# Repeated targets of a graph kernel's scatters: merged window by window instead of once at the end

## The chip, the cores and the metric

The kernel runs on one core of one Trainium2 chip. The metric is device time in microseconds, from the start of the program to its end. The profile shows one execution on that core, with one row for each instruction of TensorE (PE, with its weight loads PEld), VectorE (DVE), ScalarE (ACT), GpSimd (POOL) and SyncE (SP, which issues most DMAs here).

## The reference

One layer of a graph network over 6,250 nodes with 128 features and 200,000 edges. Every edge has a source row `idx_i = src`, a neighbour `idx_j = dst` (sorted), 20 attributes and a weight.

```python
h = maximum(layernorm(x), 0)
xw = h @ W_in
W_ij = (ssp(f_ij @ W_f1 + b_f1) @ W_f2 + b_f2) * f_ij_cutoff   # ssp(v) = softplus(v) - log 2
x_ij = xw[idx_j] * W_ij                                         # one row of 128 per edge
out = segment_sum(x_ij, idx_i, 6250)
return x + ssp(out @ W_o1 + b_o1) @ W_o2 + b_o2
```

The gather by `dst` is easy, since `dst` is sorted. The sum by `src` is the work of this case: `src` is random, and 200,000 rows of 512 bytes have to be added into 6,250 rows.

## The kernel before

**Iterations.** Edges come in chunks of 128 and quads of four chunks; there are 391 quads. The program is written out as one long list of iterations, `for i in range(...)` (L1125); in iteration `i` quad `i` gets its first layer, quad `i-1` its second, and so on. Besides this regular work, hooks are placed by hand: `at(i, point, function, ...)` (L912) puts a call into iteration `i` at one of the points `L` (loads, first), `D0`, `D1`, `A0`, `A1`, `DM`, `PE2`, `A2`, `D2` and `S` (scatters, last). Each engine then has its instructions in exactly this order, and waits on semaphores where another engine is late.

**The regular part.** `s1_pe` is the first layer on PE; `s1_exp` and `s1_ln` its softplus on ACT; `s1_guard` (L447, DVE) makes the activation `a`; `s2_pe_x` and `s2_pe_w` are the gather as a one-hot product (`xg`) and the second layer (`W`, L470); `s2_copy` (L475, ACT) makes `xc`; `s2_m` (L485, DVE) multiplies the two to the edge rows.

**Three ways to sum by `src`.** 168 of the quads are *sorted*: their rows are permuted into 16 groups on PE (`permute`) and summed into an accumulator in SBUF (`unit_pe`, a burst of 96 matmuls in the iterations called units). Rows that do not fit a group go to an overflow tile, two quads of which are summed and scattered by `over_...` (`over_scatter`, at point `S`). The other 223 quads are *scattered*: GpSimd issues one indirect DMA with add for each chunk of 128 rows (`scatter`, L547), into one of four accumulators in DRAM (`acc0` to `acc3`, taken in turn). [...]

- *Plain* quads (the first 12 and the last 19 scattered ones) compare all pairs (`s1_eq`), add repeats up on PE (`s3_pe`), copy the sums out (`s3_copy`, ACT), and send all but one of each to a trash row.
- *Listed* quads (192, numbers `LB = 12` to `LE = 204` among the scattered ones) do without that. For a window of `SW = 16` quads (64 chunks; 12 windows) the kernel compares one window ahead: `l_eq` (L364, DVE) compares two quads at a time, `l_count` (L373, PE, point `PE2`) counts with falling weights, `l_dup` marks every row that repeats an earlier one of its chunk. `l_index` (L383) then numbers the marked rows of each partition with a running sum that goes on from window to window, and gives the `j`-th marked row of partition `p` the target `ACC_R + 128 (j-1) + p`: a row in a list of `LCAP = 24` blocks of 128 rows behind each accumulator. So the scatter of a listed chunk never hits a row twice.

**The merges.** Behind the listed quads the 24 blocks are added into their real rows. `l_id(j)` (L403, DVE, one pass over 768 columns) finds which node each row of block `j` belongs to. Then, for one block an iteration: `l_dg` (ACT) and `over_row` (PE, L696) spread the ids over a row, `l_same` (L423, DVE) compares, `l_load` brings the block of all four accumulators (four DMAs on SP), `l_sum` (L429, L430, PE) adds what belongs to the same node, `l_copy` (L435, ACT) puts it into an `os` tile (two buffers, shared with the overflow), `l_ji` (L440, L441) and `over_int` (L720) make the index, and `over_scatter` scatters 128 rows. The first block is started at iteration `lend + 8 = 368`, the last scattered at 401; the last quad is number 390. Rows beyond the 24 blocks would set a flag (`l_drop`), and their chunks would be done over behind the loop.

**What is zeroed.** The lists (25 blocks with a trash block, 3,200 rows behind each accumulator) are zeroed in the first 20 iterations by 20 DMAs on SP (`zero_list`), beside the accumulators themselves.

**The end.** The last 64 scatters leave out `acc0`, so that it can be added into SBUF early (`r0_load`, `r0_tp`, `r0_add`). Behind the loop the other three accumulators are loaded (L1265), added up, and the output layer runs over 13 groups of rows.

Of the kernel before, what the change touches and what calls it, by code (L numbers as in the profile page):

```python
# [7 lines left out]
F32 = mybir.dt.float32  # L8
BF16 = mybir.dt.bfloat16
# [11 lines left out]
P = 128  # L21
# [16 lines left out]
LCAP = 24  # L38
LR = P * (LCAP + 1)
# [15 lines left out]
def tile_gnn(ctx: ExitStack, tc: tile.TileContext, x, fB, cT, srcT, srcr, dstr, win_, wf1, wf2, bias, bo1c, wo1,  # L55
# [22 lines left out]
    ZL = 5  # L78
# [15 lines left out]
    for j in range(LCAP if LE else 0):  # L94
        scat[lend + 10 + 5 * j // 4] += 1
# [62 lines left out]
    lrow = con[:, 15:16]  # L158
# [200 lines left out]
    jd_all = dropT[:, 4 * LB:4 * LE]  # L359
# [22 lines left out]

    def l_index(w):  # L383
        n0 = 4 * (LB + SW * w)
        dup = lst.pop(("dup", w))
        j = sp_.tile([P, 4 * SW], F32, tag="lj", name="lj", bufs=2)
        first = lst["j", w - 1][:, 4 * SW - 1:] if w else 0.0
        nc.vector.tensor_tensor_scan(j, dup, dup, first, op0=ALU.add, op1=ALU.max)
        lst["j", w] = j
        u = sp_.tile([P, 4 * SW], F32, tag="lu", name="lu", bufs=1)  # L390
        nc.vector.tensor_scalar(u, j, float(P), float(P * (LCAP + 1)), op0=ALU.mult, op1=ALU.min)
        nc.vector.scalar_tensor_tensor(u, u, lrow, dup, op0=ALU.add, op1=ALU.mult)
        ji = sp_.tile([P, 4 * SW], I32, tag="lji", name="lji", bufs=2)
        nc.vector.tensor_tensor(ji, u, srcT_sb[:, n0:n0 + 4 * SW], op=ALU.max)
        lst["ji", w] = ji
        nc.vector.tensor_tensor(jd_all[:, 4 * SW * w:4 * SW * (w + 1)], j, dup, op=ALU.mult)

    def l_drop():
        nc.vector.tensor_scalar(jd_all, jd_all, float(LCAP), None, op0=ALU.is_gt)

    def l_id(j):
        t = wk.tile([P, 4 * (LE - LB)], BF16, tag="pr", name="lsel", bufs=1)
        nc.vector.scalar_tensor_tensor(t, jd_all, float(j + 1), srcT_sb[:, 4 * LB:4 * LE], op0=ALU.is_equal,  # L403
                                       op1=ALU.mult, accum_out=idl[:, j:j + 1])
# [396 lines left out]
    with tc.manual_schedule():  # L801
# [102 lines left out]
        idl = cp.tile([P, LCAP], F32, name="idl")  # L904
# [7 lines left out]
        def at(i, point, fn, *a):  # L912
            hooks.setdefault((i, point), []).append((fn, a))
# [133 lines left out]
        for w in range((LE - LB) // SW):  # L1047
            for g in range(4):
                n = LB + SW * (w - 1) + 4 * g
                i = splain[n] + 2 if w else 6 + 2 * g  # L1050
                for k in range(2):
                    kk = (LB + SW * w + 4 * g) // 2 + k
                    at(max(0, i + k - 2), "L", sb_load, kk)
                    at(i + k, "DM", l_eq, kk)
                i = clear(i + 1, units)
                at(i, "PE2", l_count, (LB + SW * w) // 4 + g)
                at(i + 1, "D0", l_dup, w, g)
            at(i + 1, "D0", l_index, w)
            last_i = i + 1
        if LE:  # L1060
            for k in range(NACC):
                for j in range(ZL):
                    at((0, 5, 10, 15)[k] + j + 1, "L", zero_list, k, j)
            at(last_i + 3 + LCAP, "D2", l_drop)
            for j in range(LCAP):
                at(last_i + 2 + j, "D2", l_id, j)
                i = clear(lend + 8 if j == 0 else i + 1, units)
                assert last_i + 2 + j < i
                at(i, "L", l_start, j)
                at(i, "A0", l_dg, j)  # L1070
                at(i, "PE2", over_row, ("L", j))
                at(i + 1, "D0", l_same, j)
                k = clear(i + 1, units)
                at(k - 1, "L", l_load, j)
                at(k, "PE2", l_sum, j)
                at(k + 1, "A0", l_copy, j)
                at(k + 1, "DM", l_ji, j)
                at(k + 1, "A2", over_int, ("L", j))
                at(k + 1, "S", over_scatter, ("L", j))
        for q in mpq:  # L1080
# [19 lines left out]
            if mpi[q] % 2 or q == mpq[-1]:  # L1100
# [10 lines left out]
                at(k + 1, "S", over_scatter, q)  # L1111
        last = mpq[-1]
        for r in range(len(mpq) // RND):
            for s, k in enumerate(unit_slots(mpq, r)):
# [6 lines left out]
                  l_count, l_sum)  # L1121
# [3 lines left out]
        for i in range(max(NQ + 7, last + 14, r0_end + 2, lend + 60)):  # L1125
# [262 lines left out]
def clear(i, busy, n=1):  # L1388
    while any(i + k in busy for k in range(n)):
        i += 1  # L1390
    return i
# [30 lines left out]
def _layout(inputs):  # L1422
# [27 lines left out]
    con[:, 15] = np_ + lane  # L1450
# [53 lines left out]
```

## Time and profile before

| what | us |
|---|---|
| three runs | 2256.68, 2262.07, 2265.48 (median 2262.07) |
| the profiled execution | 2264.35 |
| its span, first to last instruction | 2262.4 |
| PE, DVE, ACT, POOL busy | 1938.6, 1840.8, 1721.4, 1661.8 |
| mean granted TensorE clock | 0.944 of full speed |

An engine's row in a grouped view gives the source line, the engine, the operation, output and inputs, the count; then busy time in us and the mean of one in ns; then how long the engine had been idle just before, and whose end released it. A wait row says which engine and line waited for which, and then total us, number of waits, longest.

### The profile page before, as it was taken

The numbers are of one execution on the slowest core, as the hardware profiler recorded it, in microseconds if no ns is written. First come the engines' busy times: TensorE is split into PE (matmuls) and PEld (weight loads), VectorE is DVE, ScalarE is ACT, GpSimd is POOL, SyncE is SP. The second block draws the span as 40 slices with busy tenths as digits, with TensorE's granted clock in tenths as the row PEclk, the third lists the DMA queues.
The fourth block names the chain that finished last, engine by engine and source line by source line (L and its number), as shares of the span: only waits on it lengthen the run. The fifth ranks groups of instructions, "written<-read, shape, count | busy, mean of one in ns | idle before, by whom it ended". The sixth has DMA issues, their size and how long they took to land. (4 is left out here: it accounts for less than half of the span.)

```text
span 2262.4 us, 58115 instructions
## 1 busy us (share of the span) xinstructions
PE 1938.6 (86%) x20425; PEld 1342.8 (59%) x20425; DVE 1840.8 (81%) x4566; ACT 1721.4 (76%) x4509; POOL 1661.8 (73%) x1052
## 2 busy tenths in 40 slices
PE   3588889989898998888898999889998989988766
PEld 2456566666566666666665666666665656666644
DVE  4678889888888988979889798897987999966544
ACT  3578778878887878878788888788887888866514
POOL 3678888877777777776777787787787787666664
PEclk9789999999999999999999999999999999999987
DMA  7897666665656565656665666665656665565558
GB/s 244 229 233 135 108 119 122 114 125 100 117 110 118 104 130 103 122 110 116 116 115 102 115 112 106 111 119 98 127 100 115 109 102 99 111 110 112 98 84 228
DMA packets 390983, 279.94 MB, mean 124 GB/s; under 512 B 98815, under 2 KB 350122, under 8 KB 390690
## 3 DMA queue, kind: packets, MB, share of 16 engines
q0 software_dynamic: 145456, 72.09, 31.9%
q1 hardware_dynamic: 244946, 204.05, 31.2%
q8 instruction: 161, 2.64, 0.5%
q14 instruction: 132, 1.08, 0.2%
q10 hardware_dynamic: 288, 0.07, 0.0%
HBM read 157.60 MB, written 118.44 MB: 122 GB/s over the span
## 5 line engine op out<-in xcount | busy, mean ns | idle before, releaser
L547 POOL DMA_INDIRECT acc<-s,lji x768 | 1247.0, 1624 | 291.5 <-issue 179.6
L652 PE MATMUL pq<-pt,pm 128*128 128x387 bf16 x2688 | 552.2, 350 | 46.6 <-DVE pt L641 17.4
L475 ACT ACTIVATE xc<-xg,cb 128x128 f32<-128x128 f32 x1564 | 446.1, 372 | 85.3 <-PE xg L462 68.9
L470 PE MATMUL W<-w,a 128*128 128x128 f32 x3128 | 469.7, 295 | 0.1
L746 PE MATMUL un<-so,mst 32*128 32x392 bf16 x8064 | 390.7, 331 | 60.0 <-ACT os L711 33.8
L658 ACT CAST mst<-pq 128x387 bf16<-128x387 f32 x672 | 299.6, 480 | 158.2 <-PE pq L652 137.8
L470 PEld LDWEIGHTS W<-w,a 128*128 128x128 f32 x3128 | 393.8, 198 | 43.2 <-issue 4.5
L652 PEld LDWEIGHTS <-pm 128*128 128x128 bf16 x2688 | 265.9, 101 | 248.6 <-issue 47.1
L746 PEld LDWEIGHTS <-mst 32*128 32x128 bf16 x8064 | 245.3, 94 | 199.4 <-issue 112.9
L447 DVE SCALAR_TENSOR_TENSOR a<-z,e 128x512 f32<-128x512 f32 x391 | 266.2, 681 | 56.6 <-ACT e L319 46.1
L319 ACT ACTIVATE e<-e,con 128x512 f32<-128x512 f32 x391 | 282.3, 722 | 12.7
L547 POOL DMA_INDIRECT acc<-os,oji x108 | 174.4, 1615 | 156.0 <-ACT pt L647 118.4
L547 POOL DMA_INDIRECT acc<-s,ji x123 | 198.9, 1617 | 103.1 <-ACT ji L528 45.7
L313 ACT ACTIVATE e<-z 128x512 f32<-128x512 f32 x391 | 239.9, 614 | 28.9 <-PE z L308 18.6
L314 ACT ACTIVATE e<-e 128x512 f32<-128x512 f32 x391 | 246.4, 630 | 12.4
L641 DVE TENSOR_TENSOR pt<-pt 128x512 f32<-128x512 f32 x336 | 231.7, 690 | 5.8
L627 DVE TENSOR_SCALAR pm<-iot,pos 128x576 bf16<-128x576 f16 x672 | 220.6, 389 | 0.0
L757 DVE TENSOR_TENSOR accT<-un,accT 128x392 f32<-128x392 f32 x320 | 158.5, 557 | 65.5 <-PE xg L462 34.8
L485 DVE TENSOR_TENSOR s<-W,xc 128x512 f32<-128x512 f32 x192 | 131.6, 685 | 83.7 <-ACT xc L475 59.6
L731 DVE TENSOR_SCALAR so<-iot,mst 128x392 bf16<-128x392 f16 x672 | 190.8, 343 | 7.7 <-PE un L746 7.7
L308 PE MATMUL z<-ft,ws 123*128 123x512 bf16 x391 | 152.1, 390 | 30.0 <-DVE mo L903 9.0
L462 PE MATMUL xg<-wn,oh 63*128 63x128 bf16 x1564 | 158.7, 223 | 13.8 <-DVE a L447 7.0
(183 smaller groups left out, 2726.8 us busy)
## 6 DMA issues: line engine op xcount, KB each, us to landing
rb<-reld SPq DMA_DIRECT2D x391, 64.0 KB
fsd<-f SPq DMA_DIRECT2D x49, 480.0 KB
ft<-fsd SPq DMA_DIRECT2D x195, 120.0 KB
sb<-src SPq DMA_DIRECT2D x169, 128.0 KB
fb<-in_fB_dram SPq DMA_DIRECT2D x49, 320.0 KB
ft<-fsd SPq DMA_DIRECT2D x195, 80.0 KB
acc<-accT SPq DMA_DIRECT2D x40, 320.0 KB
wn<-tab SPq DMA_DIRECT2D x782, 15.8 KB
```

The costliest lines, as they stand in the source:

```text
L313: nc.scalar.activation(e, st[q]["z"], AF.Abs)
L314: nc.scalar.activation(e, e, AF.Exp, scale=-1.0)
L319: nc.scalar.activation(e, e, AF.Ln, bias=half, scale=0.5)
L447: nc.vector.scalar_tensor_tensor(a, st[q]["z"], 0.0, st[q]["l"], op0=ALU.max, op1=ALU.add)
L470: nc.tensor.matmul(W[:, c, :], st[q]["a"][:, c * P:(c + 1) * P], w2, start=False, stop=(c == 3))
L475: nc.scalar.mul(xc[:, c, :], st[q]["xg"][:, c, :], late["c", q // CQ][:, 4 * (q % CQ) + c:4 * (q % CQ) + c + 1])
L547: nc.gpsimd.indirect_dma_start(out=accs[k][:rows, :], out_offset=bass.IndirectOffsetOnAxis(ap=ji, axis=0), in_=s, in_offset=None, compute_ ...
L627: nc.vector.tensor_scalar(pm[:, c], iot[:, :SLOTS], rk[r]["pos"][:, 4 * j + c:4 * j + c + 1], None, op0=ALU.is_equal)
L641: nc.vector.tensor_tensor(pt[:, :, k * P:(k + 1) * P], a, high(a), op=ALU.subtract)
L652: nc.tensor.matmul(t[:, :PW], mp[q]["pm"][:, c, s * P:(s + 1) * P], high(mp[q]["pt"][:, c:c + 1, :PW])[:, 0], start=(c == 0), stop=(c == 3))
L658: nc.scalar.copy(mp[q]["ms", s][:, :PW], mp[q].pop(("q", s))[:, :PW])
L746: nc.tensor.matmul(ts[g][:, :GN], mp[q]["ms", s][v, k * P:(k + 1) * P], mp[q]["oh"][v], start=(q == qs[0] and k == 0), stop=(q == qs[-1] a ...
```

## The change

Every window of 16 listed quads now has one block of its own, of 128 rows, that is filled without gaps, and is merged soon after the window is scattered.

- *Numbering.* `l_scan` sums the marks of a window along each partition, from zero in each window; `l_before` adds up on PE (a triangular matrix times the partitions' totals) how many marked rows the partitions before have; the row is the sum of both. `l_index` keeps a row in the block if the block has room (128 rows) and the partition has at most `LCAP = 7`; others go to the trash row and set the flag.
- *Ids.* `l_id(w)` picks a partition's marked ids, seven passes over 64 columns; `l_place` puts them in their places in the block with seven matmuls against a shifted one-hot (`oh`), in two parts of bfloat16; `l_take` adds the parts up.
- *Merges.* Twelve instead of 24, by the same functions, the merge of a window started 12 iterations after its last quad (iterations 56 to 372), its scatter at 59 to 375. A window's scatters declare only the rows up to their own block, and later windows' blocks lie lower.
- *Lists.* 12 blocks, zeroed by 12 DMAs in the first 12 iterations.
- *One iteration later* stand `l_count` (with `l_dup`) and every `over_scatter`, those of the sorted quads' overflow included. `l_index` of a window stands one to two iterations later than before.

The diff, without the constants that only follow from it:

```diff
-LCAP = 24
-LR = P * (LCAP + 1)
+LCAP = 7
...
-    ZL = 5
+    ZL = 3
...
-    for j in range(LCAP if LE else 0):
-        scat[lend + 10 + 5 * j // 4] += 1
+    NW = (LE - LB) // SW
+    LR = P * NW
+    wend = [splain[LB + SW * (w + 1) - 1] for w in range(NW)]
+    for w in range(NW):
+        scat[wend[w] + 16] += 1
...
+    def l_base(w):
+        return ACC_R + P * (NW - 1 - w)
...
+    def l_scan(w):
+        dup = lst["dup", w]
+        j = sp_.tile([P, 4 * SW], F32, tag="lj", name="lj", bufs=1)
+        nc.vector.tensor_tensor_scan(j, dup, dup, 0.0, op0=ALU.add, op1=ALU.max)
+        jd = sp_.tile([P, 4 * SW], BF16, tag="ljd", name="ljd", bufs=1)
+        nc.vector.tensor_tensor(jd, j, dup, op=ALU.mult)
+        tot = sp_.tile([P, 1], BF16, tag="ltot", name="ltot", bufs=1)
+        nc.vector.tensor_copy(tot, j[:, 4 * SW - 1:])
+        lst["j", w], lst["jd", w], lst["tot", w] = j, jd, tot
+
+    def l_before(w):
+        t = ps.tile([P, 512], F32, tag="B", name="lpre", bufs=4)
+        nc.tensor.matmul(t[:, 0:1], tri, lst.pop(("tot", w)), start=True, stop=True)
+        lst["pre", w] = t
+
     def l_index(w):
         n0 = 4 * (LB + SW * w)
-        dup = lst.pop(("dup", w))
-        j = sp_.tile([P, 4 * SW], F32, tag="lj", name="lj", bufs=2)
-        first = lst["j", w - 1][:, 4 * SW - 1:] if w else 0.0
-        nc.vector.tensor_tensor_scan(j, dup, dup, first, op0=ALU.add, op1=ALU.max)
-        lst["j", w] = j
-        u = sp_.tile([P, 4 * SW], F32, tag="lu", name="lu", bufs=1)
-        nc.vector.tensor_scalar(u, j, float(P), float(P * (LCAP + 1)), op0=ALU.mult, op1=ALU.min)
-        nc.vector.scalar_tensor_tensor(u, u, lrow, dup, op0=ALU.add, op1=ALU.mult)
+        dup, j, pre = lst.pop(("dup", w)), lst.pop(("j", w)), lst.pop(("pre", w))[:, 0:1]
+        row = sp_.tile([P, 4 * SW], F32, tag="lrow", name="lrow", bufs=1)
+        nc.vector.tensor_scalar(row, j, pre, None, op0=ALU.add)
+        oh = sp_.tile([P, P + LCAP + 1], BF16, tag="loh", name="loh", bufs=1)
+        nc.vector.tensor_scalar(oh[:, :P + LCAP], iotl, pre, None, op0=ALU.is_equal)
+        bad = sp_.tile([P, 4 * SW], F32, tag="lbad", name="lbad", bufs=1)
+        nc.vector.tensor_scalar(bad, row, float(P), None, op0=ALU.is_gt)
+        nc.vector.scalar_tensor_tensor(bad, j, float(LCAP), bad, op0=ALU.is_gt, op1=ALU.max)
+        nc.vector.tensor_scalar(row, row, float(l_base(w) - 1), None, op0=ALU.add)
+        nc.vector.scalar_tensor_tensor(j, row, trash, bad, op0=ALU.subtract, op1=ALU.mult)
+        nc.vector.tensor_tensor(row, row, j, op=ALU.subtract)
+        nc.vector.tensor_tensor(row, row, dup, op=ALU.mult)
         ji = sp_.tile([P, 4 * SW], I32, tag="lji", name="lji", bufs=2)
-        nc.vector.tensor_tensor(ji, u, srcT_sb[:, n0:n0 + 4 * SW], op=ALU.max)
-        lst["ji", w] = ji
-        nc.vector.tensor_tensor(jd_all[:, 4 * SW * w:4 * SW * (w + 1)], j, dup, op=ALU.mult)
-
-    def l_drop():
-        nc.vector.tensor_scalar(jd_all, jd_all, float(LCAP), None, op0=ALU.is_gt)
-
-    def l_id(j):
-        t = wk.tile([P, 4 * (LE - LB)], BF16, tag="pr", name="lsel", bufs=1)
-        nc.vector.scalar_tensor_tensor(t, jd_all, float(j + 1), srcT_sb[:, 4 * LB:4 * LE], op0=ALU.is_equal,
-                                       op1=ALU.mult, accum_out=idl[:, j:j + 1])
+        nc.vector.tensor_tensor(ji, row, srcT_sb[:, n0:n0 + 4 * SW], op=ALU.max)
+        nc.vector.tensor_tensor(dropT[:, n0:n0 + 4 * SW], bad, dup, op=ALU.mult)
+        lst["ji", w], lst["oh", w] = ji, oh
+
+    def l_id(w):
+        n0 = 4 * (LB + SW * w)
+        jd = lst.pop(("jd", w))
+        own = sp_.tile([P, LCAP], F32, tag="lown", name="lown", bufs=1)
+        t = wk.tile([P, 4 * SW], BF16, tag="pr", name="lsel", bufs=1)
+        for k in range(LCAP):
+            nc.vector.scalar_tensor_tensor(t, jd, float(k + 1), srcT_sb[:, n0:n0 + 4 * SW], op0=ALU.is_equal,
+                                           op1=ALU.mult, accum_out=own[:, k:k + 1])
+        two = sp_.tile([P, LCAP, 2], BF16, tag="ltwo", name="ltwo", bufs=1)
+        nc.vector.tensor_copy(two[:, :, 0], own)
+        nc.vector.tensor_tensor(two[:, :, 1], own, two[:, :, 0], op=ALU.subtract)
+        lst["two", w] = two
+
+    def l_place(w):
+        t = ps.tile([P, 512], F32, tag="B", name="lid", bufs=4)
+        oh, two = lst.pop(("oh", w)), lst.pop(("two", w))
+        for k in range(LCAP):
+            o = LCAP - 1 - k
+            nc.tensor.matmul(t[:, 0:2], oh[:, o:o + P], two[:, k], start=(k == 0), stop=(k == LCAP - 1))
+        lst["lid", w] = t
+
+    def l_take(w):
+        nc.vector.tensor_reduce(idl[:, w:w + 1], lst.pop(("lid", w))[:, 0:2], axis=AX.X, op=ALU.add)
...
-            o = ACC_R + j * P
+            o = l_base(j)
...
-                scatter(st[q]["m"][:, c, :P], lst["ji", w][:, 4 * k + c:4 * k + c + 1], ACC_R + LR)
+                scatter(st[q]["m"][:, c, :P], lst["ji", w][:, 4 * k + c:4 * k + c + 1], l_base(w) + P)
...
-                i = clear(i + 1, units)
+                i = clear(i + 2, units)
                 at(i, "PE2", l_count, (LB + SW * w) // 4 + g)
                 at(i + 1, "D0", l_dup, w, g)
+            i += 1
+            at(i, "D0", l_scan, w)
+            i = clear(i, units)
+            at(i, "PE2", l_before, w)
             at(i + 1, "D0", l_index, w)
-            last_i = i + 1
+            at(i + 2, "D2", l_id, w)
+            i = clear(i + 3, units)
+            at(i, "PE2", l_place, w)
+            at(i + 1, "D0", l_take, w)
+            i = clear(wend[w] + 12, units)
+            at(i, "L", l_start, w)
+            at(i, "A0", l_dg, w)
+            at(i, "PE2", over_row, ("L", w))
+            at(i + 1, "D0", l_same, w)
+            k = clear(i + 1, units)
+            at(k - 1, "L", l_load, w)
+            at(k, "PE2", l_sum, w)
+            at(k + 1, "A0", l_copy, w)
+            at(k + 1, "DM", l_ji, w)
+            at(k + 1, "A2", over_int, ("L", w))
+            at(k + 2, "S", over_scatter, ("L", w))
...
-                    at((0, 5, 10, 15)[k] + j + 1, "L", zero_list, k, j)
-            at(last_i + 3 + LCAP, "D2", l_drop)
-            for j in range(LCAP):
-                at(last_i + 2 + j, "D2", l_id, j)
-                i = clear(lend + 8 if j == 0 else i + 1, units)
...
-                at(k + 1, "S", over_scatter, ("L", j))
+                    at((0, 3, 6, 9)[k] + j + 1, "L", zero_list, k, j)
...
-                at(k + 1, "S", over_scatter, q)
+                at(k + 2, "S", over_scatter, q)
```

More of the change, by code (lines that the diff above doesn't have):

```diff
@@ L157, in tile_gnn @@
     off = con[:, 14:15]
-    lrow = con[:, 15:16]
     def zero_piece(eng, k, j, parts=1):
@@ L1124, in tile_gnn @@
         s1_pe(0)
-        for i in range(max(NQ + 7, last + 14, r0_end + 2, lend + 60)):
+        for i in range(max(NQ + 7, last + 16, r0_end + 2, lend + 24)):
             if i % 2 == 0 and i // 2 + 2 <= (NQ - 1) // 2:
```

20 lines of the change are left out of this document (5 added, 15 removed).

## The prediction, made before the changed kernel had run

> **What bounds the kernel now.** I read the profile's page first, then the busy time of each engine stretch by stretch, then the same stretches for one line that runs once a quad, and last what the end of the span waits for. Span and engines:
>
> ```profile
> span 2262.4 us, 58115 instructions
> PE 1938.6 (86%) x20425; PEld 1342.8 (59%) x20425; DVE 1840.8 (81%) x4566; ACT 1721.4 (76%) x4509; POOL 1661.8 (73%) x1052
> ```
>
> The span is 2262.4 us and no engine is full. The next two views have the same four stretches. In the first the pairs after the length are busy time of PE, PEld, DVE, ACT and POOL, then the granted clock:
>
> ```profile
> 380.00:1790.00 1410.00, 1268.96 (x13950) 866.13 (x13948) 1222.94 (x3022) 1148.29 (x3000) 1068.22 (x660) 0.96 0.62 113
> 1480.00:1632.00 152.00, 139.43 (x1570) 95.07 (x1568) 135.33 (x323) 127.13 (x332) 120.79 (x75) 0.98 0.62 110
> 1800.00:1924.00 124.00, 113.49 (x1260) 75.48 (x1260) 118.01 (x288) 102.02 (x268) 101.32 (x61) 0.97 0.59 102
> 1966.00:2149.00 183.00, 151.74 (x1473) 113.61 (x1472) 113.13 (x296) 123.91 (x351) 122.54 (x79) 0.93 0.58 109
> ```
>
> In the second only the guard (L447, on DVE) is counted, one for each quad of 512 edges:
>
> ```profile
> 380.00:1790.00 1410.00, 183.05 (x269) 0.96 0.62 113
> 1480.00:1632.00 152.00, 20.34 (x30) 0.98 0.62 110
> 1800.00:1924.00 124.00, 16.53 (x25) 0.97 0.59 102
> 1966.00:2149.00 183.00, 16.85 (x25) 0.93 0.58 109
> ```
>
> The middle of the kernel (380 to 1790 us) does 269 quads in 1410 us, 5.24 us each; PE is busy 90%, DVE 87%, ACT 81%, POOL 76%. Three engines in lockstep: PE is nearest to the bound, DVE close behind, POOL has room. Two later stretches tell the two apart. From 1480 to 1632 a quad takes 5.07 us with 4.65 us of PE and 4.51 of DVE; from 1800 to 1924 it takes 4.96 us with 4.54 of PE and 4.72 of DVE. More VectorE work and less TensorE work made the quad shorter. From 1966 to 2149 a quad takes 7.3 us and PE is down to 83%: here something else bounds. It is the 24 merges of repeats (L418 to L443 and their scatters), which all stand in iterations 368 to 401:
>
> ```profile
> L547 POOL DMA_INDIRECT acc<-s,ji x75 | 117.5, 1567 | 46.4 <-ACT ji L528 25.9 <-issue 18.0 <-DMA acc<-s,ji 1.9
> L547 POOL DMA_INDIRECT acc<-os,oji x30 | 46.5, 1550 | 33.0 <-ACT oji L720 16.0 <-ACT pt L647 9.8 <-issue 3.7
> ACT os L435 <- DMA acc<-os,oji: 33.6, 7, 15.2
> PE un L746 <- ACT os L435: 15.7, 4, 7.9
> 2205.91 4.12 DMA acc<-os,oji
> 2210.05 0.36 SPq L1265
> ```
>
> The first two rows are POOL from 1966 to 2210 us: 105 scatters, of which 24 are merges. They are busy 117.5 + 46.5 us, with 18.0 + 3.7 us of issue, so 1.77 us a scatter and 186 us of the 244. The next two are waits: ACT stood 33.6 us before merge copies (L435) until an earlier `os` tile had been scattered, since `os` has two buffers, and PE stood 15.7 us behind those copies. The last two are on the chain that ended last: the scatter of the last merge, and the final loads, which start when it has landed. So the merges set the end.
>
> **The change part by part.** The sum is made against the profiled execution, 2264.35 us, 2.3 us above the median of the runs (2262.07). Durations:
>
> ```profile
> L403 DVE SCALAR_TENSOR_TENSOR lsel<-dropT,srcT_sb 128x768 bf16<-128x768 bf16 x24 | 22.7, 947 | 0.0
> L403 DVE DVE_READ_ACCUMULATOR lsel<-dropT,srcT_sb 128x1 f32 x24 | 1.9, 80 | 0.0
> L388 DVE TENSOR_TENSOR_SCAN lj<-ldup,lj 128x64 f32<-128x64 f32 x11 | 4.0, 359 | 0.4
> L391 DVE TENSOR_SCALAR lu<-lj 128x64 f32<-128x64 f32 x12 | 2.9, 242 | 0.4
> L392 DVE SCALAR_TENSOR_TENSOR lu<-lu,con,ldup 128x64 f32<-128x64 f32 x12 | 3.5, 288 | 0.4
> L394 DVE TENSOR_TENSOR lji<-lu,srcT_sb 128x64 int32<-128x64 f32 x12 | 2.7, 224 | 0.4
> L396 DVE TENSOR_TENSOR dropT<-lj,ldup 128x64 bf16<-128x64 f32 x12 | 2.6, 218 | 0.0
> L423 DVE TENSOR_SCALAR leq<-orow,idl 128x128 f32<-128x128 f32 x24 | 8.2, 342 | 5.8 <-PE orow L696 5.7
> L440 DVE TENSOR_SCALAR ojd<-idl,con 128x1 f32<-128x1 f32 x24 | 4.8, 202 | 0.0
> L441 DVE SCALAR_TENSOR_TENSOR ojd<-os,con,ojd 128x1 f32<-128x1 f32 x24 | 5.3, 220 | 21.6 <-ACT os L435 19.2 <-DVE ojd L440 0.4
> L373 PE MATMUL lcnt<-wgtb,eql 128*128 128x1 bf16 x768 | 30.9, 164 | 80.9 <-DVE eql L364 74.8 <-issue 4.3 <-DVE accT L757 1.4
> L429 PE MATMUL lsum<-lm,leq 128*128 128x128 f32 x192 | 27.1, 280 | 2.5 <-DMA lm<-acc 2.0 <-issue 0.3
> L430 PE MATMUL lsum<-con,leq 128*128 128x1 f32 x48 | 6.7, 210 | 0.0
> L696 PE MATMUL orow<-ldg,onesf 128*128 128x128 f32 x48 | 11.1, 314 | 0.0
> L418 ACT ACTIVATE ldg<-idt,idl 128x128 f32<-128x128 f32 x24 | 9.5, 397 | 0.2
> L435 ACT COPY os<-lsum 128x129 f32<-128x129 f32 x24 | 6.2, 258 | 48.4 <-DMA acc<-os,oji 33.6 <-PE lsum L430 14.8
> L720 ACT ACTIVATE oji<-ojd,con 128x1 int32<-128x1 f32 x108 | 32.3, 306 | 33.2 <-DVE ojd L716 26.8 <-DVE ojd L441 2.8 <-issue 2.2
> ```
>
> 1. Tail. 24 merges behind the loop become 12, one a window, 12 iterations after the window's end. In iterations that correspond to 1966 us and later only the last window's stands, so POOL has 105 - 23 = 82 scatters there: 82 x 1.77 = 145 us. Of the 53.6 us that it waited (25.9 for the plain quads' ACT `ji`, 16.0 + 9.8 for ACT at `os` scatters, 1.9 for a DMA) the 25.9 belongs to work that stays; of the other 27.7 I keep half. That makes 145 + 26 + 14 = 185 for 244: **-59 us**. At least 23 x 1.77 = 41 goes (every wait stays), at most 244 - 145 = 99 (none stays). What is late next is still POOL, with the 19 plain quads of the end (75 scatters), and then the final loads, whose chain does not change.
>
> 2. Merges in the middle. Eleven of them cost PE (27.1 + 6.7 + 11.1) / 24 = 1.87 us each, and the new `l_before` and `l_place` eight narrow matmuls a window, priced by the count's (30.9 / 768 = 0.04 us of PE each): 0.32. Eleven times 2.19 is 24 us of PE. A quad's time over its PE time is 1410 / 1269 = 1.11, so **+27**; hidden altogether it would be 0.
>
> 3. VectorE's new work. Per window: scan 0.36, product 0.22, one column copied 0.20; `l_index` has ten operations for five: three tensor_scalar at 0.242, two scalar_tensor_tensor at 0.288, four tensor_tensor at about 0.22, and the one-hot row of 135 between 0.242 and 0.342, say 0.29, 2.5 in all; `l_id` seven selects at 0.288 + 0.08 and two small ones at 0.2, 3.0; `l_take` 0.2; `l_same` and `l_ji` 0.76. That is 7.2 us, less the old `l_index` of 1.33: 5.9 a window, 70 us over twelve. What it costs lies between nothing (the two stretches above: more DVE, no more time) and all of it (DVE at 87% has 187 us idle in the middle, most of it waiting for ACT and PE). The two stretches speak for the low end, but the new operations come in bursts of 2.5 and 3 us and stand beside the compares, where DVE is already full; I take 0.4: **+28**.
>
> 4. The 24 wide selects `l_id` (22.7 + 1.9 us of DVE, in iterations 333 to 356) go: at the same 0.4 **-10**, between 0 and 25.
>
> 5. Counts one iteration later. Today PE waits in front of them for the second compare:
>
> ```profile
> PE lcnt L373 <- DVE eql L364: 74.8, 29, 3.8
> L364 DVE TENSOR_TENSOR eql<-sb,srcT_sb 128x1024 bf16<-128x1024 int16 x96 | 116.5, 1213 | 19.1 <-DMA sb<-src 19.1
> ```
>
> The 74.8 us in 29 waits cannot recur in that place, because the compare is then an iteration old. But the compare (1.2 us, 96 times) stays on DVE, and what PE needs next is late by it too: the guard `a` of the next quad stands behind it. Between 0 and 75 us; I take a third, **-25**.
>
> 6. Zeroing of the lists: 20 pieces of 320 KB (half of the 40 in the last row below; 6.55 MB) become 12 of 256 KB (3.15 MB), all in the first iterations, where DMA is the busiest thing:
>
> ```profile
> 100.00:150.00 50.00, 36.27 (x263) 26.61 (x264) 37.94 (x86) 35.93 (x96) 37.15 (x21) 0.77 0.90 229
> DVE eql L364 <- DMA sb<-src: 19.1, 6, 8.4
> acc<-accT SPq DMA_DIRECT2D x40, 320.0 KB
> ```
>
> At 229 GB/s the 3.4 MB are 15 us of transfer (DMA share 0.90, the number before the last); what waits for loads there is above all the compare (19.1 us), so between 0 and 15: **-5**.
>
> 7. Costed at nothing: the merges' ACT operations in the middle (0.397 + 0.258 + 0.306 us, 11 times: 10.6 us if ACT's 19% idle did not cover them), their POOL scatters (11 x 1.77 = 19 us, under POOL's 24% idle), and the overflow scatters an iteration later. Queued behind those on POOL are plain and listed scatters, which now no longer wait for `oji`. SP loses 48 loads and 8 zero pieces. A merge's four loads stand in SP's queue ahead of the next quads' loads, and wait for the last scatters of their own window, ten iterations (52 us) old by then: no wait.
>
> Sum: -59 + 27 + 28 - 10 - 25 - 5 = **-44 us**, so 2264 - 44 = **2220 us**.
>
> **The rivals.**
>
> *VectorE becomes the bound in the middle.* Then its added time is paid in full, the selects' return is full too, and the counts give nothing: -59 + 27 + 70 - 25 - 0 - 5 = +8, 2272 us, no change. For it: DVE is at 87% before anything is added. Against it: the stretch from 1800 to 1924 us, with DVE at 95% (118.0 of 124), is no slower. [...]
>
> *The counts' wait is returned in full and VectorE's additions are hidden.* -59 + 27 + 0 - 0 - 75 - 5 = -112, 2152 us. For it: time followed PE in the two stretches, and the wait is idle time of PE. Against it: DVE runs on while PE stands there, and PE's next input comes from it.
>
> *ACT stands before `os` in every window: slower.* `os` keeps two buffers, and every scatter that frees one is now an iteration later. If a merge and two overflow sums come close together, ACT waits for POOL; seven such waits cost 33.6 us, 4.8 each. Two in each of eleven windows cost 106 us: -44 + 106 = +62, 2326 us. It decides once the third copy comes before the first one's scatter has landed. Against it: in the written order the third copy is at least three iterations (16 us) behind that scatter, and POOL in the middle is idle a quarter of the time.
>
> *The change doesn't do what it says:* the plain quads alone keep POOL at the end, and only the 41 us of scatters go. The sum is then -26, 2238 us, inside the forecast's own range.
>
> **How the numbers follow.** The forecast has 0.73, with 2238 in it, its own range 2185 to 2250; VectorE as the bound 0.12; the full return 0.10; ACT before `os` 0.05. Half a per cent (11 us) is about what a measurement of this kernel can tell from no change. The forecast and the full return are faster: 0.83; VectorE as the bound is the same, 0.11 with 0.01 of it beyond; slower 0.06. The range runs from 2165 to 2262: it leaves out most of the full return below and half of VectorE's case with all of ACT's above, under 2 in 10. The ends of the single terms would reach further (-99 in the tail, +70 on DVE), but not together.
>
> **What would show it.** Right: from the guard of quad 366 on, quads take under 6 us for 7.3; the last scatter of POOL belongs to a plain quad and is followed by the same 50 us of final loads; the wait of `lcnt` for `eql` falls from 74.8 to under 15 us; DVE's busy time is up by 20 to 30 us over the whole span (+70 with the twelve new merges, -25 for the selects, -18 for the 24 old merges at 0.76), PE's down by about 20. Wrong: a quad in the middle takes 5.4 us or more instead of 5.24 (0.16 us over 270 quads is 43 us, the whole gain), `os` copies that wait for scatters there, or PE waiting for `a` as long as it waited for `lcnt`.

## The result, and the profile after

| | median us | runs from - to |
|---|---|---|
| kernel before | 2259.38 | 2255.26 - 2265.48 |
| changed kernel | 2160.60 | 2157.51 - 2165.61 |

The ratio is 0.9563, 95% interval 0.9532 to 0.9593: 99 us faster, where 44 were forecast. 2160.6 us lies 4 us below the range given (2165 to 2262). The first lines of the profile's page, to be held against the first fence of the prediction:

```profile
span 2162.8 us, 58140 instructions
PE 1889.9 (87%) x20377; PEld 1314.9 (61%) x20377; DVE 1846.0 (85%) x4782; ACT 1707.1 (79%) x4473; POOL 1635.6 (76%) x1040
```

PE is busy 49 us less (forecast: about 20 less), DVE only 5 us more (forecast: 20 to 30 more). Where the time went is best read from the guard, which runs once a quad. In the two fences below the span is cut where quads 60, 330 and 360 begin, and where the last scatter of POOL ends; only the guard is counted, and the numbers behind it are the granted clock, the DMA share and GB/s. First the kernel before:

```profile
0.00:376.51 376.51, 40.92 (x60) 0.90 0.74 172
376.51:1790.12 1413.61, 183.73 (x270) 0.96 0.62 113
1790.12:1933.72 143.60, 20.42 (x30) 0.98 0.60 102
1933.72:2207.45 273.73, 21.14 (x31) 0.92 0.57 105
```

Then the changed kernel, cut at the same quads:

```profile
0.00:374.41 374.41, 40.86 (x60) 0.91 0.72 165
374.41:1764.74 1390.33, 183.75 (x270) 0.98 0.64 117
1764.74:1902.89 138.15, 20.45 (x30) 0.99 0.65 109
1902.89:2105.15 202.26, 21.16 (x31) 0.96 0.58 102
```

The beginning gains 2 us, the 270 quads of the middle 23, the 30 quads in which the wide selects stood 5, the tail 71; behind the last scatter come 58 us (2162.8 - 2105.15) for 55. So the tail is the larger part. But the 270 quads of the middle were forecast some 30 us *longer* (+27 + 28 - 25; the -10 belongs to the 30 quads behind them), and became shorter although eleven merges were put ahead of the tail. That is where the forecast failed.

The tail by POOL's rows, from the guard of quad 366 to the end of the scatters (1936 to 2107 us), against the 105 scatters and 53.6 us of waits in the prediction's second fence:

```profile
L585 POOL DMA_INDIRECT acc<-s,ji x74 | 116.1, 1569 | 38.8 <-issue 18.3 <-ACT ji L566 14.9 <-DMA acc<-s,ji 2.3
L585 POOL DMA_INDIRECT acc<-os,oji x8 | 12.4, 1544 | 2.4 <-issue 1.5 <-DMA acc<-s,ji 0.9
```

There are 82 scatters, as forecast. They are busy 116.1 + 12.4 us with 18.3 + 1.5 of issue: 148 us (forecast 145). Of waits only 14.9 + 2.3 + 0.9 = 18 us are left, where the forecast kept 40. POOL's last scatters stand back to back (start, length, and what came before):

```profile
2101.76 1.54 POOL L585 DMA_INDIRECT acc<-s,ji  x1 [0.31 <-issue]
2103.61 1.54 POOL L585 DMA_INDIRECT acc<-os,oji  x1 [0.30 <-issue]
```

The last one is a sorted quad's overflow (`os`), not a plain quad's as forecast; from the start of one to the start of the next are 1.85 us. From quad 366 to 390, 25 quads take 132 us, 5.3 us each, counted as in the prediction (forecast: under 6).

### The profile page after: what moved, and what is told of

It reads as the page before. It is cut to its first block, busy times and chain, and to the rows that moved or that the text cites. A ratio compares the mean times of both kernels' runs of the same rounds, so it can differ in the third digit from the quotient of the medians.

```text
span 2162.8 us, 58140 instructions
## 1 busy us (share of the span) xinstructions
PE 1889.9 (87%) x20377; PEld 1314.9 (61%) x20377; DVE 1846.0 (85%) x4782; ACT 1707.1 (79%) x4473; POOL 1635.6 (76%) x1040
## 4 chain that ended last, share of the span: by engine, by line
PE 44%; DVE 22%; ACT 17%; DMA 6%; issue 6%; POOL 3%; SPq 2%; DVEq 0%; ACTq 0%; POOLq 0%
PE pq L690 12%; PE un L784 11%; PE W L508 9%; ACT xc L513 4%; ACT e L315 3%; ACT e L314 3%; POOL acc L585 2%; DMA acc<-s,ji 2%; ACT mst L696 2%; DVE pm L665 2%; DVE eql L367 2%; DVE a L485 2%; DVE pt L679 2%; ACT e L320 2%; DVE accT L795 2%
## 5 line engine op out<-in xcount | busy, mean ns | idle before, releaser
L690 PE MATMUL pq<-pt,pm 128*128 128x387 bf16 x2688 | 535.7, 342 | 48.2 <-DVE pt L679 23.0
L784 PE MATMUL un<-so,mst 32*128 32x392 bf16 x8064 | 385.5, 328 | 43.4 <-ACT os L749 27.1
L690 PEld LDWEIGHTS <-pm 128*128 128x128 bf16 x2688 | 259.9, 99 | 242.1 <-issue 32.0
L784 PEld LDWEIGHTS <-mst 32*128 32x128 bf16 x8064 | 250.0, 94 | 173.0 <-issue 92.6
L314 ACT ACTIVATE e<-z 128x512 f32<-128x512 f32 x391 | 239.7, 613 | 28.6 <-PE z L309 20.5
L315 ACT ACTIVATE e<-e 128x512 f32<-128x512 f32 x391 | 246.4, 630 | 12.4
L585 POOL DMA_INDIRECT acc<-os,oji x96 | 154.0, 1604 | 31.1 <-issue 14.3
L500 PE MATMUL xg<-wn,oh 63*128 63x128 bf16 x1564 | 157.1, 222 | 13.4 <-DVE a L485 5.9
```

The lines of the kernel that those rows point to most:

```text
L314: nc.scalar.activation(e, st[q]["z"], AF.Abs)
L315: nc.scalar.activation(e, e, AF.Exp, scale=-1.0)
L585: nc.gpsimd.indirect_dma_start(out=accs[k][:rows, :], out_offset=bass.IndirectOffsetOnAxis(ap=ji, axis=0), in_=s, in_offset=None, compute_ ...
L690: nc.tensor.matmul(t[:, :PW], mp[q]["pm"][:, c, s * P:(s + 1) * P], high(mp[q]["pt"][:, c:c + 1, :PW])[:, 0], start=(c == 0), stop=(c == 3))
L784: nc.tensor.matmul(ts[g][:, :GN], mp[q]["ms", s][v, k * P:(k + 1) * P], mp[q]["oh"][v], start=(q == qs[0] and k == 0), stop=(q == qs[-1] a ...
```

## The experiments

One theory: the counts' wait was worth far more than a third of its 74.8 us. Its rival: the middle is shorter for another reason (merges, ids and VectorE's work hidden; the overflow scatters; the zeroing), and the counts gave about the 25 us forecast. All ratios below are against the kernel before on the same chip; that kernel's median was 2248.16, 2244.72 and 2263.02 us in the three sets, so rows of different sets are compared by ratios, or by single quads. The last two columns are lengths read from the guard as above, each in one profiled execution.

| label | median us | ratio, 95% interval | quads 60 to 330 | quad 360 to last scatter |
|---|---|---|---|---|
| changed kernel | 2160.60 | 0.9563 (0.9532 - 0.9593) | 1390.3 | 202.3 |
| b_late_counts | 2164.45 | 0.9622 (0.9594 - 0.9650) | 1323.7 | 276.4 |
| b_fill | 2215.27 | 0.9855 (0.9836 - 0.9874) | 1374.3 | 275.6 |
| a_early_counts | 2208.65 | 0.9828 (0.9811 - 0.9844) | 1431.0 | 202.3 |
| a_no_merges | 2086.01 | 0.9282 (0.9266 - 0.9299) | 1324.0 | 201.4 |
| a_merges_at_end | 2150.29 | 0.9573 (0.9537 - 0.9609) | 1350.4 | 240.0 |
| a_early_over | 2146.73 | 0.9560 (0.9519 - 0.9601) | 1377.5 | 202.0 |
| a_clear_sums | 2142.67 | 0.9542 (0.9505 - 0.9579) | 1370.9 | 201.6 |
| a_spread | 2159.43 | 0.9615 (0.9579 - 0.9651) | 1388.7 | 201.7 |
| a_again | 2164.54 | 0.9563 (0.9541 - 0.9585) | 1396.2 | 202.6 |
| a_spread_clear | 2163.59 | 0.9561 (0.9540 - 0.9582) | 1399.8 | 202.0 |
| a_spread_clear_early | 2168.18 | 0.9572 (0.9546 - 0.9598) | 1395.2 | 201.6 |

### The counts alone, and taken back

`b_late_counts` is the kernel before with one edit:

```diff
-                i = clear(i + 1, units)
+                i = clear(i + 2, units)
                 at(i, "PE2", l_count, (LB + SW * w) // 4 + g)
```

> The kernel before with one part of the change alone: the counts (and the marks behind them) one iteration later. By the prediction's term (-25 us) 2234 us against 2259, ratio 0.989; the middle loses little because VectorE, full beside the compares, is late next. By the theory formed from the two traces (the wait of PE for the compare cost more than itself, because the granted clock halves behind it: 123 us at half clock between 150 and 1790 us before, 65 after) about -70 us, 2190 us, ratio 0.97, and the half-clock time in the middle falls to 65 us or less. The rival, that the additions in the middle were hidden and the counts are worth what was predicted, gives the first number.

Measured: 0.9622, 84 us less. The tail is as before (276.4 us for 273.7); the gain is in the middle, and the granted clock there is 0.99 for 0.96:

```profile
370.76:1694.45 1323.69, 183.80 (x270) 0.99 0.68 121
```

The first theory holds, and goes beyond its own 70 us and the forecast's bound: 84 us (79 to 91 by the interval) came back for a wait of 74.8.

`a_early_counts` is the changed kernel with this one edit undone.

> The changed kernel with the counts back by one iteration, where they stood before. By the prediction's term +25 us on 2161: 2186 us, ratio 0.967 to the kernel before. By the theory of wait and clock +70: 2230 us, ratio 0.987, with some 75 us of PE waiting for the compare again and 120 us at half clock.

Measured: 0.9828, that is 0.0265 or 60 us above the changed kernel, and the wait is back in full:

```profile
PE lcnt L376 <- DVE eql L367: 74.5, 30, 5.3
```

```profile
379.21:1810.16 1430.95, 183.86 (x270) 0.96 0.64 113
```

So the count's move is worth 84 us by itself and 60 with the rest of the change in place. It has a counterpart: the rest of the middle's additions costs less while the wait stands (below).

### Why more came back than PE had waited

Here is one such wait in the kernel before, stretch by stretch (busy time of PE, PEld, DVE, ACT, POOL; then the clock):

```profile
494.00:497.00 3.00, 3.00 (x30) 2.05 (x27) 3.00 (x7) 2.94 (x8) 2.39 (x3) 1.00 0.84 173
497.00:500.00 3.00, 0.09 (x4) 0.00 (x0) 3.00 (x8) 2.44 (x6) 2.39 (x3) 0.86 0.62 119
500.00:503.00 3.00, 2.99 (x17) 1.31 (x18) 2.97 (x9) 0.48 (x1) 2.69 (x2) 0.50 0.77 158
503.00:507.00 4.00, 4.00 (x29) 3.52 (x30) 0.99 (x3) 1.89 (x6) 3.39 (x3) 0.63 0.81 164
```

And PE's own lines in it (start, length; the bracket is the idle time before):

```profile
493.72 1.56 PE L652 MATMUL pq<-pt,pm 128*128 128x387 bf16 x8
...
500.01 0.37 PE L373 MATMUL lcnt<-wgtb,eql 128*128 128x1 bf16 x8 [2.92 <-DVE eql L364]
500.24 2.75 PE L652 MATMUL pq<-pt,pm 128*128 128x387 bf16 x8
```

PE stands 2.92 us before `lcnt`. Behind the wait the clock is 0.50 for the next 3 us and not full until 506, and the same eight permutes take 2.75 us instead of 1.56. In the clock records of the middle (380 to 1680 us) the kernel before has 21 stretches at half clock, 3.4 or 6.8 us long, 88.7 us together; 19 of them begin in or just behind an idle of PE of 1.8 to 3.5 us, 17 of these at `lcnt`. Not every such idle has one: 5 of the 24 idles over 1.8 us have none, one of 3.09 us among them. `b_late_counts` has 6 stretches with 23.9 us, `a_early_counts` 21 with 99.0, the changed kernel 11 with 54.6 (from 150 to 1790 us, where the expectation above has 65, it has 68).

To tell the clock from the wait, `b_fill` keeps the wait and its place, but gives PE useless matmuls to do during it (into columns that nobody reads; `FILL` is a number for each of 29 counts):

```diff
+            for _ in range(FILL.get(g - LB // 4, 0) if k else 0):
+                nc.tensor.matmul(t[:, P:], onesb, b2rep.rearrange("k c f -> k (c f)")[:, :3 * P], start=True, stop=True)
```

> The kernel before with its counts where they were, but in the 29 counts that waited over 1 us TensorE gets filler matmuls (128x384, results unused) ahead of the second compare, 5 for each us of wait. The work stays the same, and PE waits as long as before for the same compare, only busy. If the halved clock behind the waits costs time by itself: half-clock time in the middle falls from 123 us to about 55, which is 34 us of PE time, so 2225 to 2240 us, ratio 0.985 to 0.99. If only the wait costs: 2259 to 2270 us, ratio 1.0 to 1.005.

Measured: 0.9855, 33 us less with *more* work and the same order. A filled wait (the first line is the filler) and the waits left:

```profile
487.47 2.44 PE L374 MATMUL lcnt<-b2rep,onesb 128*128 128x384 bf16 x14
490.53 0.35 PE L376 MATMUL lcnt<-wgtb,eql 128*128 128x1 bf16 x8 [0.63 <-DVE eql L365]
490.75 1.56 PE L655 MATMUL pq<-pt,pm 128*128 128x387 bf16 x8
```

```profile
PE lcnt L376 <- DVE eql L365: 15.9, 28, 1.1
```

```profile
368.71:1742.98 1374.27, 183.82 (x270) 0.99 0.66 116
```

The eight permutes behind it take 1.56 us, and between 380 and 1680 us 7 stretches at half clock with 27.3 us are left: 61.4 less than before. Behind the unfilled wait 1.19 of the permutes' 2.75 us at a clock of 0.50 are lost against these 1.56, 43%. Taking half of all half-clock time as lost, an estimate from that clock, the 61.4 us give some 31 (27 with the 43%), near the 33 measured. Then about 33 us of the 84 are the clock alone; that the other 51 are the wait itself is a difference, not a measurement. PE did not come to stand before the guard's `a` in place of the counts, which the prediction feared: the second layer waits 0.0 us in `b_late_counts` (L470) and 0.2 in the changed kernel. What grew is the permutes' wait for `pt`, from 17.4 to 31.5 us in `b_late_counts`. The page of the changed kernel:

```profile
L508 PE MATMUL W<-w,a 128*128 128x128 f32 x3128 | 466.4, 294 | 0.2 <-DVE a L485 0.2
```

### The merges: what they cost where

`a_no_merges` skips ids, placement and merges of the first eleven windows:

```diff
             at(i + 1, "D0", l_index, w)
+            if w < NW - 1:
+                continue
```

> The changed kernel without the ids and merges of the first eleven windows (selects, placing, the row, the four loads, sums, index and scatter), so repeats of these windows are left out of the result; numbering and scatters into the blocks stay. It prices what the change put into the middle. By the prediction (PE at 1.11 for 2.15 us a window, VectorE at 0.4 for 4.0 us a window) 26 + 18 = 44 us less: 2117 us, ratio 0.937. If these additions are hidden: 2155 to 2161 us, ratio 0.955. If VectorE were paid in full: 2091 us, ratio 0.926.

Measured: 0.9282, 63 us below the changed kernel, and the middle is as long as with late counts alone, 1324.0 us for 1323.7:

```profile
363.35:1687.39 1324.04, 183.81 (x270) 1.00 0.68 121
```

Two things follow. Ids and merges cost 63 us, where the forecast had 27 for the merges and, of VectorE's 28, some 14 for the ids. And the new numbering (`l_scan`, `l_before`, the longer `l_index`), which stays in this kernel, costs next to nothing: one quad of a window is 2 to 3 us longer than with late counts alone, its neighbours are shorter by nearly as much, and some 0.4 us a window are left.

A part of the 63 us may be the clock again: between 380 and 1680 us this kernel has 10.2 us at half clock and the changed kernel 54.6, and half of the difference, by the same estimate, is 22 us. No run separates it from the work, as `b_fill` does for the counts.

`a_merges_at_end` keeps ids and placement where they are and puts the twelve merges behind the listed quads, where the 24 were:

```diff
-            i = clear(wend[w] + 12, units)
+            i = clear(lend + 8 if w == 0 else last_l + 1, units)
+            last_l = i
```

Its overflow scatters stand an iteration earlier, as in `a_early_over` below, which ran in the same set and is the one to compare with.

> The changed kernel's twelve dense blocks, merged one an iteration behind the listed quads (from iteration 368), as the 24 were before; overflow and merge scatters stand one iteration earlier, as before. By the prediction (tail 59 us for 23 merges, 2.6 each; the middle pays 30 us for eleven) the two nearly cancel: 2159 us, ratio 0.956. By the runs so far (tail 71 us for 23 merges, 3.1 each; the middle pays 49 us beside the ids) 2146 us, ratio 0.950, with 44 us less between quads 60 and 330 and 34 us more behind quad 360.

Measured: 0.9573, no different from the changed kernel: the prediction's 0.956, and not the 0.950 that the runs so far had suggested. Middle and tail of this kernel:

```profile
365.14:1715.58 1350.44, 183.31 (x270) 0.99 0.67 118
...
1850.72:2090.71 239.99, 21.10 (x31) 0.93 0.58 101
```

The tail is 38 us longer than with the merges in the middle (240.0 for 202.0), and everything ahead of quad 360 is 34 us shorter: it begins at 1850.7 us for `a_early_over`'s 1884.5. What the merges' new place saves at the end it costs in the middle. Of the tail's 71 us, 34 are there because there are twelve merges and not 24 (273.7 to 240.0).

The ids: against `a_no_merges`, quad for quad by the starts of the guard, the quad in which `l_id` stands is 2.1 to 2.4 us longer in `a_merges_at_end`, in each of the windows 1 to 10. Their rows in the changed kernel (60 to 1900 us):

```profile
L426 DVE SCALAR_TENSOR_TENSOR lsel<-ljd,srcT_sb 128x64 bf16<-128x64 bf16 x84 | 18.9, 225 | 2.5
L426 DVE DVE_READ_ACCUMULATOR lsel<-ljd,srcT_sb 128x1 f32 x84 | 6.8, 81 | 0.0
```

These means must not be added up, for the read of the accumulator starts while its select still runs. The start and the end of one burst, in order of time:

```profile
150.88 0.22 DVE L426 SCALAR_TENSOR_TENSOR lsel<-ljd,srcT_sb 128x64 bf16<-128x64 bf16 x1
151.02 0.09 DVE L426 DVE_READ_ACCUMULATOR lsel<-ljd,srcT_sb 128x1 f32 x1
151.14 0.23 DVE L426 SCALAR_TENSOR_TENSOR lsel<-ljd,srcT_sb 128x64 bf16<-128x64 bf16 x1
...
152.95 0.17 DVE L430 TENSOR_TENSOR ltwo<-lown,ltwo 128x7 bf16<-128x7 f32 x1
```

From its first start to its last end a window's burst takes 2.24 to 2.33 us, and 2.1 to 2.4 are paid: nearly all of it, where I took 0.4. The numbering grew from 1.3 to 3.1 us of VectorE a window (its rows added up; from 1.2 to 2.6 with overlaps counted once) at next to no cost. It stands at the point `D0` and the ids at `D2`; whether the point decides was not tried.

### Where single merges cost 6 to 8 us

Against `a_no_merges` three quads of the changed kernel stand out: 59, 85 and 229 are 8.0, 6.4 and 7.6 us longer, 22 us together. Quad 85 (window 1) by the waits of 495 to 512 us, and PE's lines there:

```profile
ACT mst L696 <- PE pq L690: 8.3, 4, 5.4
DVE a L485 <- ACT e L320: 7.6, 1, 7.6
...
PE lsum L467 <- DVE leq L461: 2.3, 1, 2.3
```

```profile
499.03 1.21 PE L467 MATMUL lsum<-lm,leq 128*128 128x128 f32 x8 [2.29 <-DVE leq L461]
...
503.40 3.79 PE L690 MATMUL pq<-pt,pm 128*128 128x387 bf16 x12 [0.57 <-ACT mst L696]
```

```profile
495.00:512.00 17.00, 13.50 (x121) 8.71 (x123) 9.17 (x26) 8.25 (x25) 8.20 (x6) 0.80 0.54 105
```

The sum waits 2.29 us for its compare, the mean clock of the stretch is 0.80 (the clock records have 6.8 us at half clock from 499.9 us on, and 10.2 us at the like wait of quad 229), and behind the sum stand the permutes of an iteration just ahead of a unit, which take turns with ACT's copies over the four PSUM tiles `B` that the merge uses too. Quad 59 (window 0) is another case; the waits of 360 to 372 us:

```profile
PE un L784 <- ACT os L749: 7.1, 1, 7.1
ACT os L749 <- DMA acc<-os,oji: 6.4, 1, 6.4
```

That is the third rival's mechanism: an `os` copy before which an older `os` had not been scattered. It happens once.

`a_early_over` puts all overflow scatters back by one iteration:

```diff
-            at(k + 2, "S", over_scatter, ("L", w))
+            at(k + 1, "S", over_scatter, ("L", w))
...
-                at(k + 2, "S", over_scatter, q)
+                at(k + 1, "S", over_scatter, q)
```

> The changed kernel with the overflow's and the merges' scatters one iteration earlier, as before. The prediction costs this part at nothing: 2161 us, ratio 0.956. By its third rival (copies to os wait for a scatter that is now later; the trace has one such wait, 6.4 us in the first window) some 8 us less: 2153 us, ratio 0.953. If POOL's waits at these scatters (118 us before) mattered, it would be slower.

Measured: 0.9560 for 0.9563. The wait of quad 59 is gone (that quad is 8.0 us shorter); the time is the same within the interval.

`a_clear_sums` chooses the iteration of a merge sum so that it does not fall on a unit, on an overflow sum, or on the iteration ahead of either:

```diff
+        crowd = units | {u - 1 for u in units}
+        for q in mpq[1::2]:
+            crowd |= {clear(q + 8, units), clear(q + 8, units) - 1}
...
-            i = clear(wend[w] + 12, units)
+            i = wend[w] + 12
+            while i in units or i + 1 in crowd:
+                i += 1
...
-            k = clear(i + 1, units)
+            k = i + 1
```

> The changed kernel with its merges moved by up to eight iterations, so that a merge's sums never stand in an iteration just ahead of a unit (which puts four permutes into it), nor in the iteration of an overflow sum or the one ahead of that. Nothing else changes. The theory: merges cost 49 us in the middle, of which four (windows 0, 1, 6, 7: 6 to 10 us each) pay for PE and ACT taking turns over four PSUM banks, or for an os tile not yet scattered. Then 20 to 25 us less: 2138 us, ratio 0.946. The rival, that a merge costs what its instructions cost wherever it stands (the prediction's term): 2161 us, ratio 0.956.

Measured: 0.9542. Quads 59, 85 and 229 are 8.0, 6.2 and 7.6 us shorter than in the changed kernel, so the place made those costs; which part of it (the PSUM tiles, the clock, or the order) was not taken apart. The whole gains 0.2%, which the intervals do not resolve. The theory's 0.946 lies outside the interval and the rival's 0.956 inside: what three quads gained does not show in the total.

### Spreading the ids

`a_spread` (on top of `a_clear_sums`) does two selects in each of four iterations, and places three iterations later:

```diff
-            at(i + 2, "D2", l_id, w)
-            i = clear(i + 3, units)
+            for part in range(4):
+                at(i + 2 + part, "D2", l_id, w, part)
+            i = clear(i + 6, units)
             at(i, "PE2", l_place, w)
```

> The kernel with clear sums, and the seven selects of a window spread over four iterations, two in each, in place of one burst of 3 us; the placing stands three iterations later. VectorE does the same work. If the ids' 2 us a window are the price of the burst: some 10 to 15 us less than with clear sums alone, 2126 us, ratio 0.941. If VectorE is simply the bound there: no change against clear sums.

Measured: 0.9615, no better and rather worse. In nine windows of ten the quad with the ids is 1.6 to 2.7 us shorter (0.7 in the other). But the three quads behind it, which now hold the rest of the selects, are 0.7 to 2.2 us longer together: of 17.2 us that the ten quads gain, 14.5 come back there. In window 3, for quad 104, where the selects start, and then for the next three quads (only the guard is counted), `a_clear_sums` and then `a_spread`, all at full clock:

```profile
586.24:595.59 9.35, 0.69 (x1) 1.00 0.56 69
595.59:608.12 12.53, 2.04 (x3) 1.00 0.48 101
```

```profile
596.52:604.13 7.61, 0.69 (x1) 1.00 0.53 76
604.13:617.87 13.74, 2.04 (x3) 1.00 0.57 108
```

So the burst is not the cause: at `D2` the selects are paid nearly wherever they stand, as the rival has it. That the kernel became slower comes on top. `l_place` now fell ahead of units in some windows, and such quads grew by up to 5.2 us; and between 380 and 1680 us there are 58.5 us at half clock where `a_clear_sums` has 20.5. Half of that difference, by the same estimate, is 19 us, about the 17.8 by which the middle is longer. The mean granted clock of whole executions says the same: 0.964 to 0.969 in the four of `a_clear_sums`, 0.957 to 0.961 in the four of `a_spread`.

`a_spread_clear` places with `clear(i + 6, crowd)`; `a_spread_clear_early` also has the earlier overflow scatters; `a_again` is the changed kernel once more, in the same set.

> Clear sums and spread selects, with the placing moved on to an iteration that is neither a unit, nor just ahead of one, nor that of an overflow sum. The spread alone took the 1.6 to 2.7 us that each window's burst cost out of its iteration, and lost more where the placing then stood ahead of a unit (5.2 and 4.6 us at quads 49 and 193). If crowded iterations (banks and turns between PE and ACT) are the price: 10 to 20 us under clear sums, 2125 to 2130 us on the first chip's scale, ratio 0.943 to 0.947. If VectorE's work is paid wherever it stands: ratio 0.954, as clear sums.

> The same with the overflow's and the merges' scatters one iteration earlier, as in the kernel before. At nothing, as the prediction costs it: equal to the one ahead within 0.3%. If the wait for an os tile or POOL's order mattered beyond the one merge that has been moved by now: a difference of over 0.5%.

> The changed kernel itself, on the same chip as the next two: ratio 0.956 to the kernel before, the mark for them.

Measured: 0.9561, 0.9572 and 0.9563. The 0.943 to 0.947 of crowded iterations lie outside the interval of `a_spread_clear` (0.9540 - 0.9582), the rival's 0.954 just inside, and the earlier scatters cost nothing that shows. The large single costs are gone and the total is the same. Half-clock time between 380 and 1680 us is 51.2, 58.0 and 51.2 us in the three, so nothing was won there; what else came in place of the large costs is open. No version here is shown to beat the changed kernel.

## Why the prediction was wrong

The sign was right; 44 us were forecast and 99 came. (The time is off by 59 us, since the sum starts from the profiled execution's 2264.35 us and the kernel's median is 2259.38.) Of the 55 us, 12 are in the tail and the rest ahead of it, where one term was mis-sized. By its steps:

1. *Tail, -59 (41 to 99).* Measured -71. The scatters and their price were right (82 at 1.8 us). Of the 27.7 us of other waits I kept half; 3 stayed, and of the 26 us before `ji` only 15. The 38 us that come from the merges' place are a gain for the tail alone: `a_merges_at_end` shows them paid back in the middle.
2. *Merges in the middle, +27.* 34 with the overflow scatters early, and 8 more with the `os` wait of quad 59. 14 are in quads 85 and 229, where the sum stood ahead of a unit. The forecast had no term for the neighbours, nor for the half clock behind a merge's wait; without these three quads 20 us are left, near the 24 us of PE's work that it had.
3. *VectorE's work, +28.* The ids cost about 26 us (1350.4 - 1324.0, two sets whose kernels before differ by 0.15%), the numbering nothing that shows. The sum was right by accident: one factor of 0.4 stood for nearly 0 and nearly 1.
4. *Wide selects, -10.* `b_late_counts` takes 141.6 us for quads 330 to 360, `a_no_merges`, which has neither the wide selects nor a merge there, but the last window's ids, 135.1: -6.5. About right.
5. ***Counts, "Between 0 and 75 us; I take a third, -25".*** This step failed. Alone the move gives 84 us, with the rest 60. The taken value was too low, since I expected PE to wait for the guard's `a` in its place, and it waited 0.2 us. And the upper bound was wrong: I took the idle time of the wait for all that the wait could cost, though the half clock behind it was in the same trace; `b_fill` puts 33 us on it.
6. *Zeroing, -5.* Quad 30 begins 5.5 us earlier (209.5 us for 215.0), which agrees; no run changed the zeroing alone.
7. *At nothing.* The overflow scatters: right but for the one `os` wait of 6.4 us. ACT, POOL and the loads were not measured alone; they are in the 63 us of ids and merges.

The terms do not add. With the counts late, ids and merges cost 68 us beside the other terms (2259.4 - 71 - 5 - 7 - 84 = 2092 for 2160.6); with them early 44 (0.9828 is 39 us, for 71 + 5 + 7). The likely reason, which no run shows, is that a part of the new work was hidden while PE stood before the counts. By the clock records all the additions bring 31 us of half-clock time with late counts (54.6 for 23.9) and 10 with early ones (99.0 for 88.7).

Of the rivals, the one with the counts returned in full (2152 us, a chance of 0.10) came closest to the time, but its second half was wrong: VectorE's additions were not hidden. The rival with VectorE as the bound was far off in its time (2272 us), and VectorE is busy 1257 us of 1390 in the middle; but for the ids it was right, since they are paid nearly in full:

```profile
374.41:1764.74 1390.33, 1272.27 (x14159) 876.74 (x14156) 1257.03 (x3286) 1155.78 (x3036) 1083.74 (x671) 0.98 0.64 117
```

ACT before `os` happened once, not twice a window. Of the signs named, the quads of the tail, the missing wait at `lcnt` and the 50 to 60 us behind the last scatter came true. PE's busy time fell by 49 and not 20; 16.5 of that is that the same permutes ran faster (2688 of them took 552.2 us, 350 ns each, on the page before):

```profile
L690 PE MATMUL pq<-pt,pm 128*128 128x387 bf16 x2688 | 535.7, 342 | 48.2 <-DVE pt L679 23.0
```

DVE's busy time rose by 5 only. The lengths of all its instructions added up rose by 18.6 us, but the records overlap by 13.4 us more than before, the accumulator reads with their selects among them, and the busy time counts an overlap once.

## What to carry to other kernels

Bound the price of a wait of TensorE by its idle time *and*, as an estimate, half of the half-clock time that goes with it, and look for that in the trace of before; here the idle time alone, 74.8 us, was not the upper bound. With the estimate it is 74.8 + 32 = 107 us (the 32 are half of 88.7 - 23.9), of which 84 came back. An instruction that needs another engine's result of the same iteration is worth trying one iteration later before anything larger is built: here one changed number gave 84 us, and the whole change 99. Work that goes from a tail into a middle where three engines are busy for over 80% of the time was not free there (34 us paid ahead of quad 360 for 38 saved behind it); ask what stands in the iteration that it is put into.

## What the runs showed of the hardware

- In the kernel before, between 380 and 1680 us, 19 of 24 idles of TensorE of 1.8 to 3.5 us had 3.4 or 6.8 us at a granted clock of 0.5 begin in them or just behind them; 5 had none, and 2 of the 21 stretches came with idles of 1.4 and 1.7 us. Useless matmuls in the waits made the kernel 33 us faster.
- A VectorE burst of 2.24 to 2.33 us at the end of an iteration (`D2`) cost 2.1 to 2.4 us of time, although VectorE was idle for a tenth of the middle. Spread over four iterations it gave back 17.2 us in ten quads and took 14.5 in the quads behind.
- A select of 64 columns with an accumulated output took 225 ns. The read of the accumulator (81 ns) started about 150 ns after the select's start, and the next select some 267 ns after the one before.
